# A gated graph network and an attention layer on one core: where the loads and the preparation of the weights stand in the order of work

## The chip, the cores and the metric

The kernel runs on one core of a Trainium2 chip. The metric is the device time of one execution in microseconds, here the median of three runs.

## The reference

The input holds 64 graphs of 256 nodes with 256 features each (x) and one integer adjacency matrix per graph (adj). Layer 0 is a gated graph network of three steps, layer 1 a graph attention network with four heads; each acts on a normalized copy of x and is added to x.

```python
h = relu(layernorm(x))
for i in range(3):                                  # layer 0
    m = h @ weight[i]
    aggr = A.T @ m                                  # per graph, A = (adj != 0)
    gi, gh = aggr @ w_ih.T + b_ih, h @ w_hh.T + b_hh
    r, z = sigmoid(i_r + h_r), sigmoid(i_z + h_z)   # thirds of gi and gh
    n = tanh(i_n + r * h_n)
    h = (1 - z) * n + z * h
x = x + h
h = relu(layernorm(x))                              # layer 1
v = h @ W.T + b                                     # 4 heads of 64
logits = leaky_relu(l_src[:, None] + l_dst[None, :], 0.2), masked where adj != 1
x = x + softmax(logits) @ v
```

Here l_src and l_dst are products of v with the two halves of a.

## The kernel before

Two graphs form a pair; there are 32 pairs. The work of a pair is cut into ticks: pair p begins at tick 18 p (APART), its step l of layer 0 has its six parts tick_0 to tick_5 at ticks 12 l to 12 l + 5 after that, and attention follows from tick 32. So two or three pairs are under way at a time, except at the beginning and the end. In ticks 6 to 11 only pair 0 is under way, and it has no step then: only its update (L499), its transposes back (L546) and the sums of its new state (L381).

The order of the work is written out by hand. `at(tick, phase, p, fn)` (L307) enters a function under a tick and one of the phases STEP, READY and REST; the last loop (L777) calls them by tick and phase, the later pair first, and in the order of entry within a pair. Nothing reorders the instructions afterwards: each engine runs its own in the order in which they were issued. TensorE (PE) does the products and transposes, VectorE (DVE) and ScalarE (ACT) evict PSUM and do the elementwise work, GpSimd (POOL) some of it, SyncE (SP) issues most loads. Three PSUM banks (`bank`, L97) go round among the transposes, the aggregation and the preparation of weights, five others among the gates.

DMAs issued on SP and ACT take eight completion counters in turn, in the order in which the program issues them. A DMA whose counter has been used waits, on the engine that issues it, until the earlier DMA of this counter has landed. ACT issues DMAs from the same stream of instructions that holds its evictions.

Before the ticks begin, the kernel issues the loads of x and adj of the first pair on SP (L123), and on ACT those of w_ih, weight[0], w_hh, the other weights and the two biases (L149 to L175). PE transposes w_ih and w_hh in blocks of 128 x 128 (L169), and DVE evicts them as ih_T and hh_T (L170). From hh_T DVE makes w_h (L196, L197) and seven blocks w_n (L198 to L205). `step_weights(l)` (L207) transposes weight[l] (pmT, L212; evicted by ACT, L215), multiplies it by ih_T (pc, L220; evicted by DVE, L224) and makes of it the six blocks of w_a[l] (RA, ZA, NA, S1, S2, S4; L226 to L229), which step l uses from its tick_2 on. `step_weights(0)` stands before the ticks, `step_weights(1)` at tick 6, `value_weights` (L238) at tick 7, `step_weights(2)` at tick 8. `value_weights` loads W, b and eight pieces of a, builds a_exp (the pieces as columns among zeros), w_val and b_val for the attention, which uses them from tick 37.

Of pair 0, `plan_norm` (L310) gives statistics of x (L320), rstd (L326, L327) and the normalized xn_a (L332); `plan_relu_T` transposes it (pt_a, L351) into hT_a (L352); `first_hi` (L535) and `first_lo` (L539) split it into hNhi and hNlo; `to_edge` (L526) makes the edge matrix; `state_sums` (L381) makes T1, T3n and T2n. tick_0 aggregates (pa, L418), tick_2 has the first product with w_a (p), tick_3 and later the products pd, pc, pe and pn. In the trace the tiles T1, T2, T3 and T4 are shown as T.

Of the kernel before, what the change touches and what calls it, by code (L numbers as in the profile page):

```python
# [17 lines left out]
P = 128  # L18
# [8 lines left out]
def gated_gnn_then_gat_kernel(  # L27
# [95 lines left out]
    first = load_x(0), load_adj(0, "adj")  # L123
# [23 lines left out]


    ih_T = [buf("val", [P, G * P], f"ih_T_{k}") for k in range(KD)]  # L149
    hh_T = [buf("row", [P, G * P], f"hh_T_{k}") for k in range(KD)]  # L150
    w_msgs = []
    for name, src, dst in (("ih", w_ih, ih_T), ("hh", w_hh, hh_T)):
        if name == "hh":
            w_msgs.append(buf("hn", [P, KD, D], "w_msg_0"))
            nc.scalar.dma_start(w_msgs[0], weight[0].rearrange("(k q) e -> q k e", q=P))
        nat = buf("zz", [P, G, D], f"{name}_nat")
        for g0 in range(0, G, 3):
            nc.scalar.dma_start(
                nat[:, g0 : g0 + 3, :], src[g0 * P : (g0 + 3) * P, :].rearrange("(g q) d -> q g d", q=P)
            )  # L160
        if name == "hh":
            for l in range(1, L):
                w_msgs.append(buf("row", [P, KD, D], f"w_msg_{l}"))
                nc.scalar.dma_start(w_msgs[l], weight[l].rearrange("(k q) e -> q k e", q=P))
        for k in range(KD):
            for g0 in range(0, G, 3):
# [3 lines left out]
                nc.vector.tensor_copy(dst[k][:, g0 * P : (g0 + 3) * P], pt[:, : 3 * P])  # L170

    bi = const.tile([P, G], F32, name="bi")
    bh = const.tile([P, G], F32, name="bh")
    nc.scalar.dma_start(bi, b_ih.rearrange("(g q) -> q g", q=P))
    nc.scalar.dma_start(bh, b_hh.rearrange("(g q) -> q g", q=P))  # L175
# [18 lines left out]
    for k in range(KD):  # L194
        r_, z_, n_ = (hh_T[k][:, ts(g, D)] for g in range(3))
        nc.vector.tensor_copy(w_h[:, k, ts(RH, D)], r_)  # L196
        nc.vector.tensor_sub(w_h[:, k, ts(RZ, D)], r_, z_)  # L197
        nc.vector.tensor_scalar_mul(w_n[:, (N00, N01)[k], :], n_[:, :P], 0.5)  # L198
        nc.vector.tensor_scalar_mul(w_n[:, (NS3, N11)[k], :], n_[:, P:], 0.5)
    nb = [w_n[:, j, :] for j in range(7)]  # L200
# [6 lines left out]
    def step_weights(l):  # L207
# [8 lines left out]
        for k in range(KD):  # L216
# [12 lines left out]
            nc.vector.tensor_scalar_mul(blk[ZA], blk[ZA], -1.0)  # L229

    step_weights(0)

    w_val = const.tile([P, KD, VW], F32, name="w_val")
    b_val = const.tile([P, VW], F32, name="b_val")

# [575 lines left out]
```

## Time and profile before

| | us |
|---|---|
| median of three runs (2610.36 to 2613.37) | 2613.26 |
| the profiled execution, whole | 2612.2 |
| its span | 2610.4 |
| PE busy in it | 2539.7 (97%) |
| DVE busy | 1849.2 (71%) |
| ACT busy | 1462.2 (56%) |
| POOL busy | 653.0 (25%) |
| first matmul of the first aggregation (pa, L418) | 39.22 |
| first product with w_a (p, L293) | 46.38 |

The profile is of one execution, and its times count from the start of the span. In a timeline a row gives start, duration, engine, line, operation, output and inputs with their shapes, the number of instructions taken together (x), and in brackets how long the engine had been idle before and what released it. PEld is PE's loading of weights, which overlaps its products. ACTq and SPq are rows of the queues, which issue DMAs. PEclk is the clock that PE was granted, as a share of full speed. In a table by stages each engine has its busy time and its instructions.

### The profile page before, as it was taken

Reading aid. Unit: us, or ns where it says so; the run is one execution under the profiler, and the core shown is the slowest. Engines: PE = TensorE matmul, PEld = TensorE weight load, DVE = VectorE, ACT = ScalarE, POOL = GpSimd, SP = SyncE. Lnnn points to the kernel's source line nnn. Section 1 sums busy time; section 2 is a strip of 40 time slices with the busy share of each in tenths; the row PEclk is TensorE's granted clock in tenths of the full one; section 3 lists DMA queues with packets and bytes.
Section 4 is the critical chain, followed back from the end, with each engine's and each line's share of the span. In section 5 each row is a group of like instructions: output and inputs, shape, how many; then the busy total and the mean of one; then the engine's idle time right before and its main releaser. Section 6 shows DMA issues by size and latency. Waiting matters only on the chain.

```text
span 2610.4 us, 38818 instructions
## 1 busy us (share of the span) xinstructions
PE 2539.7 (97%) x14074; PEld 2266.0 (87%) x14074; DVE 1849.2 (71%) x4528; ACT 1462.2 (56%) x3077; POOL 653.0 (25%) x518
## 2 busy tenths in 40 slices
PE   6899999999999999999999999999999999999985
PEld 5688898888988888989888989888898888898975
DVE  4567777777776777777777777777777677777663
ACT  2346555655655665655665555565565566565553
POOL 0012222222223222222222322222222322222221
PEclk9899999999999999999999999999999999999995
DMA  3004344434344434344443334443434453433444
GB/s 89 19 9 94 89 110 98 110 85 90 82 106 98 114 84 88 92 95 106 106 98 92 84 88 110 98 111 85 90 81 106 98 114 84 89 92 86 98 98 114
DMA packets 120320, 239.89 MB, mean 92 GB/s; under 512 B 9792, under 2 KB 79424, under 8 KB 120128
## 3 DMA queue, kind: packets, MB, share of 16 engines
q0 software_dynamic: 34272, 132.13, 26.5%
q1 hardware_dynamic: 80160, 102.52, 12.9%
q10 hardware_dynamic: 5696, 2.76, 0.4%
q8 instruction: 111, 1.82, 0.3%
q14 instruction: 81, 0.66, 0.1%
HBM read 219.82 MB, written 17.56 MB: 91 GB/s over the span
## 4 chain that ended last, share of the span: by engine, by line
PE 95%; DVE 2%; DMA 1%; issue 1%; ACT 0%; POOL 0%; ACTq 0%; POOLq 0%; SPq 0%; DVEq 0%
PE pd L293 19%; PE pn L293 13%; PE pc L293 13%; PE po L749 9%; PE pa L418 7%; PE qb L396 6%; PE pe L293 6%; PE p L293 6%; PE qa L396 5%; PE pv L601 4%; PE pback L552 3%; PE pt_a L351 1%; PE pt_b L351 1%; PE plink L652 1%; PE pc L220 0%
## 5 line engine op out<-in xcount | busy, mean ns | idle before, releaser
L487 POOL TENSOR_TENSOR R<-hT_a,hn 128x512 f32<-128x512 f32 x192 | 318.3, 1658 | 883.7 <-ACT hn L484 840.9
L293 PE MATMUL pn<-aggr,w_a 128*128 128x256 f32 x1536 | 367.1, 382 | 0.0
L293 PE MATMUL pd<-T,w_a 128*128 128x256 f32 x1536 | 364.6, 380 | 0.0
L293 PEld LDWEIGHTS pn<-aggr,w_a 128*128 128x128 f32 x1536 | 287.1, 190 | 42.9 <-DVE pn L473 6.3
L293 PEld LDWEIGHTS pd<-T,w_a 128*128 128x128 f32 x1536 | 286.9, 190 | 36.9
L749 PEld LDWEIGHTS po<-val,zz 128*128 128x128 f32 x2048 | 258.7, 201 | 17.2 <-ACT zz L740 12.5
L749 PE MATMUL po<-val,zz 128*128 128x65 f32 x2048 | 255.9, 281 | 11.6 <-ACT zz L740 11.6
L689 DVE CUSTOM_DVE_ANT_0 any<-drow,noedge 128x256 f32<-128x256 f32 x512 | 244.7, 478 | 16.9 <-DMA drow<-score_dram 7.9
L762 POOL TENSOR_TENSOR x<-x,o 128x256 f32<-128x256 f32 x128 | 117.1, 915 | 498.2 <-DVE o L757 498.2
L484 ACT ACTIVATE hn<-pn,bi 128x256 f32<-128x256 f32 x384 | 160.4, 469 | 144.5 <-PE pn L293 144.4
L403 ACT ACTIVATE R<-pc,brz 128x256 f32<-128x256 f32 x192 | 80.5, 470 | 280.0 <-PE pc L293 280.0
L717 ACT ACTIVATE zz<-zz,val 128x256 f32<-128x256 f32 x512 | 231.7, 509 | 8.3 <-DMA zz<-score_dram 8.3
L502 DVE SCALAR_TENSOR_TENSOR R<-Z,R 128x512 f32<-128x512 f32 x192 | 131.8, 686 | 147.3 <-POOL R L487 142.7
L558 DVE TENSOR_TENSOR hNlo<-pback,hNhi 128x512 fp32r<-128x512 f32 x128 | 88.5, 691 | 196.2 <-ACT hNhi L557 196.2
L403 ACT ACTIVATE R<-pe,brz 128x256 f32<-128x256 f32 x192 | 80.5, 470 | 195.2 <-PE pe L293 195.2
L503 DVE SCALAR_TENSOR_TENSOR hT_a<-R,hn 128x512 f32<-128x512 f32 x192 | 175.0, 912 | 13.6 <-DVE R L502 0.5
L293 PE MATMUL pc<-hT_a,w_h 128*128 128x256 f32 x768 | 181.4, 379 | 0.0
L293 PE MATMUL pe<-aggr,w_a 128*128 128x256 f32 x768 | 181.4, 379 | 0.0
L293 PE MATMUL pc<-aggr,w_a 128*128 128x256 f32 x768 | 181.4, 379 | 0.0
L293 PE MATMUL pd<-T,w_h 128*128 128x256 f32 x768 | 181.4, 379 | 0.0
L293 PE MATMUL p<-T,w_a 128*128 128x256 f32 x768 | 181.4, 379 | 0.0
L473 DVE SCALAR_TENSOR_TENSOR pn<-R,hn 128x512 f32<-128x512 f32 x192 | 142.9, 744 | 52.0 <-ACT hn L399 27.4
(147 smaller groups left out, 5310.6 us busy)
## 6 DMA issues: line engine op xcount, KB each, us to landing
zz<-score_dram POOLq DMA_DIRECT2D x64, 1024.0 KB, 11.9
zz<-topT_dram POOLq DMA_DIRECT2D x62, 1024.0 KB, 8.1
adj<-in_adj_dram SPq DMA_DIRECT2D x64, 512.0 KB
drow<-score_dram SPq DMA_DIRECT2D x64, 512.0 KB
x<-in_x_dram SPq DMA_DIRECT2D x32, 512.0 KB
out_dram<-x SPq DMA_DIRECT2D x32, 512.0 KB
score_dram<-score SPq DMA_DIRECT2D x128, 4.0 KB
topT_dram<-topT SPq DMA_DIRECT2D x128, 2.0 KB
```

The costliest lines, as they stand in the source:

```text
L293: nc.tensor.matmul(pt[:, ts(c, N)], w[:, k, j * D + c * P : j * D + (c + 1) * P], src[:, k, :], start=start and c == 0 and k == 0, stop=(c ...
L396: nc.tensor.matmul(pt, w_n[:, j, :], src, start=start, stop=True, skip_group_check=True)
L403: nc.scalar.activation(of(dst, i)[:, c, :], src[:, c, :], AF.Tanh, bias=brz[:, g0 + c : g0 + c + 1], scale=0.5)
L418: nc.tensor.matmul(pt[:, ts(i, N)], hN[half][:, i * KN + s, ts(e, P)], edge[:, i * KN + s, :], start=(s == 0 and half == 0), stop=(s == KN ...
L473: nc.vector.scalar_tensor_tensor(by_c(self.bank(f"pn{i}")), of(self.R, i), 1.0, of(self.hn, i), op0=ALU.add, op1=ALU.mult)
L484: nc.scalar.activation(n__[:, c, :], p_n[:, c, :], AF.Tanh, bias=bi[:, 2 * KD + c : 2 * KD + c + 1])
L487: nc.gpsimd.tensor_sub(of(self.R, i), of(self.hT(), i), n__)
L502: nc.vector.scalar_tensor_tensor(d_, of(self.Z, i), 1.0, d_, op0=ALU.add, op1=ALU.mult)
L503: nc.vector.scalar_tensor_tensor(of(self.hT(), i), d_, 0.5, of(self.hn, i), op0=ALU.mult, op1=ALU.add)
L689: nc.vector.tensor_tensor_reduce(any_, drow[r // KN][:, h, :], v["noedge"][:, r, :], 1.0, -3.0e38, ALU.add, ALU.max, accum_out=v["top"][:, ...
L717: nc.scalar.activation(zz[:, h, :], zz[:, h, :], AF.Prelu, alpha=ALPHA, bias=v["val"][:, r, S0 + H + h : S0 + H + h + 1],)
L749: nc.tensor.matmul(po[:, ts(h_, VC)], logits[i][:, j, h_, ts(s, P)], v["val"][:, i * KN + j, ts(h_, VC)], start=(j == 0), stop=(j == KN - 1),)
```

## The change

The loads move ahead of everything else. SP issues x_0, w_hh, adj_0, weight[0], w_ih, weight[1], weight[2] and W, and then the later loads of x and adj; ACT issues the two biases, then b, the eight pieces of a, and b once more. POOL clears a_exp and presets b_val. The preparation of the weights becomes functions at ticks: w_hh's (`state_weights`) at tick -5, on ACT in place of DVE, with its remaining DVE part (`state_weights_2`) at tick -2; w_ih's and the transposes of weight[0] at tick 0, `step_weights(0)` at tick 1; the transposes of weight[1] at tick 5 and `step_weights(1)` at tick 6; of weight[2] at tick 13 and `step_weights(2)` at tick 14; `value_weights` at tick 20, without its loads. In `turn_gates` and `step_weights` some of the evictions go to ACT. These functions are now entered after those of the pairs, so within a phase they follow those of pair 0.

```diff
--- before.py
+++ after.py
@@ -120,7 +120,35 @@
         return xt
     ctx.enter_context(tc.manual_schedule())
-    first = load_x(0), load_adj(0, "adj")
+    def load_gates(name, src):
+        nat = buf("zz", [P, G, D], f"{name}_nat")
+        for g0 in range(0, G, 3):
+            nc.sync.dma_start(
+                nat[:, g0 : g0 + 3, :], src[g0 * P : (g0 + 3) * P, :].rearrange("(g q) d -> q g d", q=P)
+            )
+        return nat
+    def load_square(tag, name, src):
+        y = buf(tag, [P, KD, D], name)
+        nc.sync.dma_start(y, src.rearrange("(k q) e -> q k e", q=P))
+        return y
+    x_0 = load_x(0)
+    hh_nat = load_gates("hh", w_hh)
+    first = x_0, load_adj(0, "adj")
+    ih_T = [buf("val", [P, G * P], f"ih_T_{k}") for k in range(KD)]
+    hh_T = [buf("row", [P, G * P], f"hh_T_{k}") for k in range(KD)]
+    w_msgs = [load_square("Z", "w_msg_0", weight[0])]
+    ih_nat = load_gates("ih", w_ih)
+    w_msgs += [load_square("row", f"w_msg_{l}", weight[l]) for l in range(1, L)]
+    w_nat = load_square("zz", "w_nat", W)
+    bi = const.tile([P, G], F32, name="bi")
+    bh = const.tile([P, G], F32, name="bh")
+    nc.scalar.dma_start(bh, b_hh.rearrange("(g q) -> q g", q=P))
+    nc.scalar.dma_start(bi, b_ih.rearrange("(g q) -> q g", q=P))
     ident = const.tile([P, P], F32, name="ident")
@@ -144,35 +172,14 @@
     mhalf = const.tile([P, R], F32, name="mhalf")
     nc.gpsimd.memset(mhalf, -0.5)
-    ih_T = [buf("val", [P, G * P], f"ih_T_{k}") for k in range(KD)]
-    hh_T = [buf("row", [P, G * P], f"hh_T_{k}") for k in range(KD)]
-    w_msgs = []
-    for name, src, dst in (("ih", w_ih, ih_T), ("hh", w_hh, hh_T)):
-        if name == "hh":
-            w_msgs.append(buf("hn", [P, KD, D], "w_msg_0"))
-            nc.scalar.dma_start(w_msgs[0], weight[0].rearrange("(k q) e -> q k e", q=P))
-        nat = buf("zz", [P, G, D], f"{name}_nat")
-        for g0 in range(0, G, 3):
-            nc.scalar.dma_start(
-                nat[:, g0 : g0 + 3, :], src[g0 * P : (g0 + 3) * P, :].rearrange("(g q) d -> q g d", q=P)
-            )
-        if name == "hh":
-            for l in range(1, L):
-                w_msgs.append(buf("row", [P, KD, D], f"w_msg_{l}"))
-                nc.scalar.dma_start(w_msgs[l], weight[l].rearrange("(k q) e -> q k e", q=P))
+    def turn_gates(name, nat, dst, evict):
         for k in range(KD):
             for g0 in range(0, G, 3):
                 pt = bank(f"pw_{name}_{k}_{g0}")
                 for g in range(3):
                     nc.tensor.transpose(pt[:, ts(g, P)], nat[:, g0 + g, ts(k, P)], ident)
-                nc.vector.tensor_copy(dst[k][:, g0 * P : (g0 + 3) * P], pt[:, : 3 * P])
-    bi = const.tile([P, G], F32, name="bi")
-    bh = const.tile([P, G], F32, name="bh")
-    nc.scalar.dma_start(bi, b_ih.rearrange("(g q) -> q g", q=P))
-    nc.scalar.dma_start(bh, b_hh.rearrange("(g q) -> q g", q=P))
+                evict[g0 // 3](dst[k][:, g0 * P : (g0 + 3) * P], pt[:, : 3 * P])
     brz = const.tile([P, 2 * KD], F32, name="brz")
@@ -191,63 +198,76 @@
     RH, RZ = range(2)
     N00, N01, N11, NS1, NS2, NS3, NS4 = range(7)
     RA, ZA, NA, S1, S2, S4 = range(6)
-    for k in range(KD):
-        r_, z_, n_ = (hh_T[k][:, ts(g, D)] for g in range(3))
-        nc.vector.tensor_copy(w_h[:, k, ts(RH, D)], r_)
-        nc.vector.tensor_sub(w_h[:, k, ts(RZ, D)], r_, z_)
-        nc.vector.tensor_scalar_mul(w_n[:, (N00, N01)[k], :], n_[:, :P], 0.5)
-        nc.vector.tensor_scalar_mul(w_n[:, (NS3, N11)[k], :], n_[:, P:], 0.5)
-    nb = [w_n[:, j, :] for j in range(7)]
-    nc.vector.tensor_add(nb[NS1], nb[NS3], nb[N11])
-    nc.vector.tensor_sub(nb[NS2], nb[NS1], nb[N00])
-    nc.vector.tensor_sub(nb[NS3], nb[N00], nb[NS3])
-    nc.vector.tensor_sub(nb[NS4], nb[N01], nb[NS2])
-    nc.vector.tensor_scalar_mul(nb[N11], nb[N11], -1.0)
-    def step_weights(l):
-        w_msgT = buf("zz", [P, KD, D], f"w_msgT_{l}")
+    def state_weights():
+        turn_gates("hh", hh_nat, hh_T, (nc.scalar.copy, nc.scalar.copy))
+        for k in range(KD):
+            r_, z_, n_ = (hh_T[k][:, ts(g, D)] for g in range(3))
+            nc.scalar.mul(w_n[:, (N00, N01)[k], :], n_[:, :P], 0.5)
+            nc.scalar.mul(w_n[:, (NS3, N11)[k], :], n_[:, P:], 0.5)
+            nc.scalar.copy(w_h[:, k, ts(RH, D)], r_)
+    def state_weights_2():
+        nb = [w_n[:, j, :] for j in range(7)]
+        nc.vector.tensor_add(nb[NS1], nb[NS3], nb[N11])
+        nc.vector.tensor_sub(nb[NS2], nb[NS1], nb[N00])
+        nc.vector.tensor_sub(nb[NS3], nb[N00], nb[NS3])
+        nc.vector.tensor_sub(nb[NS4], nb[N01], nb[NS2])
+        nc.vector.tensor_scalar_mul(nb[N11], nb[N11], -1.0)
+        for k in range(KD):
+            nc.vector.tensor_sub(w_h[:, k, ts(RZ, D)], hh_T[k][:, :D], hh_T[k][:, D : 2 * D])
+    w_msgT = {}
+    def step_weights_T(l):
+        w_msgT[l] = buf("zz", [P, KD, D], f"w_msgT_{l}")
         pt = bank(f"pmT_{l}")
         for e in range(KD):
             for k in range(KD):
                 nc.tensor.transpose(
                     pt[:, e * D + k * P : e * D + (k + 1) * P], w_msgs[l][:, k, ts(e, P)], ident
                 )
-        nc.scalar.copy(w_msgT.rearrange("q e d -> q (e d)"), pt)
+        nc.scalar.copy(w_msgT[l].rearrange("q e d -> q (e d)"), pt)
+    def step_weights(l):
         for k in range(KD):
             for g0 in range(0, G, 3):
                 pt = bank(f"pc_{l}_{k}_{g0}")
                 for e in range(KD):
                     nc.tensor.matmul(
-                        pt[:, : 3 * P], w_msgT[:, e, ts(k, P)], ih_T[e][:, g0 * P : (g0 + 3) * P],
+                        pt[:, : 3 * P], w_msgT[l][:, e, ts(k, P)], ih_T[e][:, g0 * P : (g0 + 3) * P],
                         start=(e == 0), stop=(e == KD - 1),
                     )
-                nc.vector.tensor_copy(w_a[l][:, k, g0 * P : (g0 + 3) * P], pt[:, : 3 * P])
+                (nc.scalar.copy if g0 else nc.vector.tensor_copy)(
+                    w_a[l][:, k, g0 * P : (g0 + 3) * P], pt[:, : 3 * P]
+                )
             blk = [w_a[l][:, k, ts(j, D)] for j in range(6)]
             nc.vector.tensor_add(blk[S1], hh_T[k][:, D : 2 * D], blk[ZA])
             nc.vector.tensor_sub(blk[S2], blk[S1], hh_T[k][:, :D])
             nc.vector.tensor_sub(blk[S4], blk[RA], blk[S2])
             nc.vector.tensor_scalar_mul(blk[ZA], blk[ZA], -1.0)
-    step_weights(0)
     w_val = const.tile([P, KD, VW], F32, name="w_val")
     b_val = const.tile([P, VW], F32, name="b_val")
     a_exp = const.tile([P, KD, 2 * H], F32, name="a_exp")
+    bcol = const.tile([P, KD], F32, name="bcol")
+    nc.scalar.dma_start(bcol, b.rearrange("(k q) -> q k", q=P))
+    nc.gpsimd.memset(a_exp, 0.0)
+    for h in range(H):
+        k, q0 = divmod(h * C, P)
+        for s in range(2):
+            nc.scalar.dma_start(
+                a_exp[q0 : q0 + C, k, s * H + h : s * H + h + 1],
+                a[h : h + 1, s * C : (s + 1) * C].rearrange("o c -> c o"),
+            )
+    nc.gpsimd.memset(b_val, 1.0)
+    nc.scalar.dma_start(
+        b_val[:, :S0].rearrange("q (h c) -> q h c", h=H)[:, :, :C],
+        bass.AP(tensor=b.tensor, offset=b.offset, ap=[[0, P], [C, H], [1, C]]),
+    )
     def value_weights():
-        w_nat = buf("zz", [P, KD, D], "w_nat")
-        nc.scalar.dma_start(w_nat, W.rearrange("(k q) d -> q k d", q=P))
-        bcol = const.tile([P, KD], F32, name="bcol")
-        nc.scalar.dma_start(bcol, b.rearrange("(k q) -> q k", q=P))
-        nc.vector.memset(a_exp, 0.0)
-        for h in range(H):
-            k, q0 = divmod(h * C, P)
-            for s in range(2):
-                nc.scalar.dma_start(
-                    a_exp[q0 : q0 + C, k, s * H + h : s * H + h + 1],
-                    a[h : h + 1, s * C : (s + 1) * C].rearrange("o c -> c o"),
-                )
         nc.vector.memset(w_val, 0.0)
         for k in range(KD):
             pt = bank(f"pwv_{k}")
@@ -264,11 +284,6 @@
                     start=(g == 0), stop=(g == KD - 1),
                 )
             nc.vector.tensor_copy(w_val[:, k, S0:], pa[:, : 2 * H])
-        nc.vector.memset(b_val, 1.0)
-        nc.scalar.dma_start(
-            b_val[:, :S0].rearrange("q (h c) -> q h c", h=H)[:, :, :C],
-            bass.AP(tensor=b.tensor, offset=b.offset, ap=[[0, P], [C, H], [1, C]]),
-        )
         bmat = buf("o", [P, KD, P], "bmat")
         pb = bank("pb")
         for k in range(KD):
@@ -768,12 +783,24 @@
             rest(t, output(r))
         rest(66, lambda: nc.sync.dma_start(out_rows[ts(p, T), :].rearrange("(r q) d -> q r d", q=P), v["x"]))
-    at(SUB, REST, 0, lambda: step_weights(1))
-    at(SUB + 1, REST, 0, value_weights)
-    at(SUB + 2, REST, 0, lambda: step_weights(2))
     for p in range(NPAIR):
         plan_pair(p)
+    at(-5, REST, 0, state_weights)
+    at(-2, READY, 0, state_weights_2)
+    def input_weights():
+        turn_gates("ih", ih_nat, ih_T, (nc.scalar.copy, nc.vector.tensor_copy))
+        step_weights_T(0)
+    at(0, REST, 0, input_weights)
+    at(1, REST, 0, lambda: step_weights(0))
+    at(5, REST, 0, lambda: step_weights_T(1))
+    at(SUB, REST, 0, lambda: step_weights(1))
+    at(13, REST, 0, lambda: step_weights_T(2))
+    at(14, REST, 0, lambda: step_weights(2))
+    at(20, REST, 0, value_weights)
     for tick in sorted(plan):
         for phase in plan[tick]:
             for _, fn in sorted(phase, key=lambda y: y[0]):
```

## The prediction

> **What bounds the kernel now.** I read the busy time by stages first. It asks where TensorE (PE) is idle, since only there can a new order of the work gain.
>
> ```profile
> core 0: us, PE busy (x) PEld busy (x) DVE busy (x) ACT busy (x) POOL busy (x), PEclk, DMA share, GB/s
> 0.00:36.30 36.30, 19.22 (x72) 13.14 (x72) 16.35 (x50) 2.70 (x5) 1.83 (x9) 0.94 0.46 137
> 36.30:60.40 24.10, 22.42 (x102) 19.57 (x102) 11.57 (x25) 9.65 (x21) 1.28 (x1) 0.88 0.08 23
> 60.40:92.80 32.40, 20.54 (x74) 13.81 (x72) 16.22 (x41) 3.35 (x7) 2.24 (x2) 0.79 0.06 13
> 92.80:120.00 27.20, 27.20 (x144) 24.36 (x145) 16.66 (x29) 13.68 (x30) 2.82 (x2) 1.00 0.13 39
> ```
>
> From 92.8 us PE is busy throughout at clock 1.00, and the page's chain of waits gives PE 95% of the span. So what is saved before 92.8 us reaches the end whole, and what is added to PE later is paid whole. Before 92.8 us PE idles 17.1 + 1.7 + 11.9 us and runs partly at a low clock. The timeline says why:
>
> ```profile
> 33.72 1.38 DVE L332 TENSOR_SCALAR xn_a<-x,mv_a,rstd_a 128x256 f32<-128x256 f32 x4 [1.24 <-POOL rstd_a L327]
> 38.38 0.69 DVE L526 TENSOR_SCALAR edge<-adj 128x1024 fp32r<-128x1024 int32 x1
> 39.22 0.55 PE L418 MATMUL pa<-edge,hNhi_a 128*128 128x256 f32 x1 [1.68 <-DVE edge L526]
> 46.38 1.89 PE L293 MATMUL p<-T,w_a 128*128 128x256 f32 x8
> ...
> 69.84 5.04 ACTq L247 DMA_DIRECT2D a_exp<-in_L_gnn_a_dram  x8
> 74.16 0.57 PE L262 MATMUL pwa<-a_exp,w_nat 128*128 128x8 f32 x2 [6.33 <-DMA a_exp<-in_L_gnn_a_dram]
> ...
> 82.55 7.37 PE L220 MATMUL pc<-ih_T,w_msgT 128*128 128x384 f32 x16 [0.68 <-ACT w_msgT L215]
> 92.75 0.39 PE L418 MATMUL pa<-edge,hNlo 128*128 128x256 f32 x1 [1.33 <-DVE hNlo L558]
> ```
>
> The first aggregation (pa) starts at 39.22 us because DVE normalizes x_0 only after all weights (x_0's statistics start at 30.06). PE goes from the end of step 0 (60.41) to the aggregation of step 1 (92.75) through all remaining weights, with a wait for the 4-byte loads of a_exp. DMAs that wait for a completion counter show in ScalarE's queue:
>
> ```profile
> 5.03 3.21 ACTq L158 DMA_DIRECT2D hh_nat<-in_L_gnn_w_hh_dram  x2
> 10.68 3.39 ACTq L164 DMA_DIRECT2D w_msg<-in_L_gnn_weight_dram  x2
> 16.66 0.38 ACTq L174 DMA_DIRECT2D bi<-in_L_gnn_b_ih_dram  x1
> 17.07 0.56 ACTq L175 DMA_DIRECT2D bh<-in_L_gnn_b_hh_dram  x1
> ```
>
> By the program's waits, the first hh_nat may issue when x_0 has landed, which therefore was at 5.03. The gaps in this queue are such waits.
>
> **What the Trainium skill says.** "DMA: Bandwidth & Descriptors", section "Issuing engines are not separate DMA queues": transfers of all issuers share the same 16 DMA engines. The trace agrees: from 4 to 5 us SP's queue alone moved 0.35 MB, from 6 to 7 us the two queues 0.17 and 0.18. Its section "Queues, rings and completion order" has an engine alternate between queues packet by packet; these equal shares agree. "Perfetto Trace Analysis", section "DMA Instruction — HWDGE (DVE, Sync)": the semaphore wait lies on the issuing sequencer, ahead of the start that is reported, and the sequencer is free only after the issue. The gaps above agree; that work of ScalarE's own (ACT) queues behind such a wait, no row shows yet. "TensorE: Matmul & The Clock Gate", section "What's actually happening": half clock by default and after about 3.4 us of idleness. The products of L220 agree: loads every 0.64 us after 20.11 and again after 82.55, every 0.31 from 86.53.
>
> **Part 1, loads.** SP now issues x_0, w_hh, adj_0, weight[0], w_ih, weight[1], weight[2], W, x_1 in that order, and ACT issues b_hh, b_ih, b, eight pieces of a, and b again: 12 small DMAs ahead of its first evictions. Eight counters are used in turn, so ACT's sequencer meets these waits: b behind b_ih; the eight pieces of a behind w_hh, adj_0, both halves of w_ih, b, piece 1, weight[2], W; the last DMA behind piece 3. Then the hh_T evictions may go. I time W, the latest of them. SP's first bytes up to 3.0 us are 0.066 MB, then 0.348 MB/us. Up to W there are 3.67 MB: 3.0 + 3.60/0.348 = 13.4 us. The two bias loads are 1,536 packets, 96 per DMA engine. Packets of this kind took 21 ns of an engine alone (775 in the us from 18 to 19) at a share of 0.41, so between 0.8 and 2.0 us; I take 1.3. Receipt 1.1 us (x_1's last byte was at about 9.4 by the counts, seen at 10.68; x_0 took 0.7). W is seen at 15.8. Then one piece of a (5.04/8 = 0.63) and 0.38 for the last: ACT is free at c = 16.8 us, 15 to 20 with the ends (a late b_hh also holds the second half of w_ih on SP).
>
> **Part 2, up to the first aggregation.** From c, on ACT: four copies of 384 columns (0.48 each, between 0.39 for 256 and 0.59 for 512; the fourth waits for PE's transposes into a bank that the first frees, 0.87) 1.9 us, four products and two copies 1.4, hT_a, hNhi and the hand over 1.6. On DVE: hNlo 1.14, the five small operations of w_n 1.08 (22.01 to 23.09), two subtractions 0.66, edge to pa 0.84. Sum 8.6: pa at 25.4. x_0's normalization now waits for b_ih (brz comes first on DVE; seen by 10.4) and then takes 5.0 us (30.06 to 35.1), done by 16: hidden behind ACT.
>
> **Part 3, within step 0.** From pa to p (the first product with w_a) are 7.16 us now. PE gets in between 12 + 4 transposes (0.54 per four) 2.2, 16 records of L220 at 0.32, 5.1, and a wait of about 0.2 for DVE's S1 of the second half, behind ACT's copy: 7.5. So p at 25.4 + 7.16 + 7.5 = 40.1 where it was at 46.38: **6.3 us gained**. If the clock falls to half in between, up to 3 less.
>
> **Part 4, between step 0 and step 1.** Up to the last product of weights 1 nothing changes on PE (60.41 to about 67.2, at the old times). DVE decides: after the update (64.44) copy 0.56, about 0.4 until ACT's copy is there, four operations 1.47; then copy 0.56, until ACT's copy at 68.0, 1.47, two hNlo 1.3: 70.75. So 10.35 us in place of 32.34: **22.0 gained**, between 20.5 and 22.5. Late next is DVE, with PE idle about 1.6 us there.
>
> **Part 5, given back.** weights 2 moves into ticks 13 and 14, where PE is full: 0.54 + 5.1 = **5.6**; its DVE and ACT parts have slack there (DVE is 61% busy from 92.8 to 120). value_weights moves to tick 20. PE's own part is about 1.8 us, but there are three banks: pwv_1 waits for the eviction of hNlo (1.6 us after the transposes), pwa_1 for the memset and copy on DVE, pb for bmat behind all of them (copies 0.42, 0.17, 0.42, 0.17, then 0.29). On PE 4.15 us pass until the next product: **4.2**, between 1.8 and 6. Queued behind PE's wait is pd of pair 1, and behind it all of PE's later work. Where DVE catches up sooner, less is paid. SP is moved past eight more issues, of x_1 at about 13 us; it lands by 19, and is first read in tick 4 (54.5 now, some 48 then): nothing. POOL's two memsets replace DVE's: nothing.
>
> **The sum.** 6.3 + 22.0 − 5.6 − 4.2 = 18.5 us. The profiled execution took 2612.2 us (span 2610.4), so it would be 2593.7; against the median of 2613.26, 1.1 above it, **2594.8 us**.
>
> **Rivals.** *A, as above: 2594.8.* *B, ACT's own work isn't held by its DMA waits*, or they end early. Then DVE decides: b_ih at 10.4, then the old 9.16 us from the statistics to pa, 1.74 more for the new operations: pa at 21.4, 4 us sooner: 2590.8; with the biases at 7 us, 2588. For it: no row shows ACT's work held. Against: the sequencer's waits in ACTq are real. *C, the moved weights cost more than their place saves*: the products at half clock (0.64, 5.1 more) and value_weights at 6 instead of 4.2: 2601.7. For it: the cold L220 rows; against: PE is at 1.00 wherever these now stand, and idle gaps of 1 us (61.2 to 62.2) left it warm. *D, slower: ACT's small DMAs run one after another*, each a full round trip. That is decided from the point at which ACT is free at 35.3 us (16.8 + 18.5). A piece of a took 2.3 us from issue to use, the second bias load 2.9; with 0.5 for contention, 12 × 3.4 + 0.75 = 41.6 us, so 6.3 us slower: 2619.6. Against: the counters chain at most three of them. *E, it does nothing:* excluded for part 4, since the wait for a_exp at 74.16 has no work left behind it; only a price in part 5 of the size of the gain could bring it about.
>
> **How the numbers follow.** A 0.61, B 0.17, C 0.13, E or a weak D within 0.2% 0.05, D 0.04. About 0.2% (5 us) is what a measurement of this kernel can tell from no change. The range 2588 to 2603 takes in A with its bounds (c 3 us later, value_weights at 1.8 or 6), B and C. Faster 0.91, same 0.05, slower 0.04.
>
> **What would show it.** ACT's first copy of hh_T between 15 and 19 us, directly after b_val's issue (B: at about 9); pa near 25, p near 40; the first wait of PE for hNlo in step 1 near 64; products of weights 2 at 0.32 us a record in a full PE; a gap of 2 us around pwv and pb at tick 20; thereafter each row about 18.5 us earlier. The prediction is wrong if the rows after 120 us move by another amount than the rows before.

## The result, and the profile after

| | before | after |
|---|---|---|
| median, us | 2612.61 (4 runs, 2610.36 to 2613.37) | 2596.09 (4 runs, 2595.86 to 2596.36) |
| profiled execution, whole / span | 2612.2 / 2610.4 | 2595.86 / 2594.1 |
| PE busy in it | 2539.7 | 2532.7 |

The ratio is 0.9938, with a 95% interval from 0.9921 to 0.9955: 16.5 us faster by the medians, 16.3 by the two spans. 2594.8 was forecast.

From L169 on most line numbers of the changed kernel are higher than before, by 11 to 20 (L293 is now L308, L418 is L433, L558 is L573). First the busy time by stages, cut where the first aggregation, the first product with w_a, the aggregation of step 1 and the end of what follows tick 20 now lie; each engine has its busy time and its instructions, then come the clock, the share of the DMA engines and GB/s.

```profile
core 0: us, PE busy (x) PEld busy (x) DVE busy (x) ACT busy (x) POOL busy (x), PEclk, DMA share, GB/s
0.00:25.60 25.60, 8.56 (x42) 6.42 (x43) 8.03 (x27) 6.81 (x16) 2.13 (x11) 1.00 0.72 210
25.60:41.00 15.40, 15.38 (x67) 12.34 (x68) 6.68 (x15) 5.01 (x10) 0.00 (x0) 1.00 0.11 35
41.00:65.00 24.00, 21.77 (x99) 17.14 (x97) 14.95 (x36) 9.05 (x21) 3.52 (x3) 1.00 0.00 1
65.00:106.00 41.00, 39.05 (x201) 33.23 (x202) 25.80 (x53) 16.87 (x36) 2.82 (x2) 1.00 0.09 26
106.00:120.00 14.00, 14.00 (x61) 12.09 (x61) 7.62 (x18) 5.44 (x14) 1.28 (x2) 0.88 0.01 1
```

Before the first aggregation PE idled 18.7 us (39.2 less 20.5 busy), now 17.0; and that stretch ends at 25.6 instead of 39.2. Between step 0 and the aggregation of step 1 the long idle is gone (2.2 us from 41 to 65). New is an idle of 2 us in 65 to 106, and a clock of 0.88 after it, in a stretch where PE is busy throughout. (The 1.00 of the first two rows leaves out what the clock's record does not cover at the beginning: up to 30.7 us the matmuls go at half rate.)

The timeline of the same kernel, at the places that were shown of before:

```profile
7.93 0.37 ACTq L255 DMA_DIRECT2D bcol<-in_L_gnn_b_dram  x1
8.01 0.16 DVE L186 TENSOR_TENSOR brz<-bi,bh 128x4 f32<-128x4 f32 x1 [6.23 <-DMA bi<-in_L_gnn_b_ih_dram]
8.41 8.00 ACTq L260 DMA_DIRECT2D a_exp<-in_L_gnn_a_dram  x8
16.50 0.54 ACTq L265 DMA_DIRECT2D b_val<-in_L_gnn_b_dram  x1
17.09 1.24 ACT L181 COPY hh_T<-pw_hh 128x384 f32<-128x384 f32 x3 [13.68 <-issue]
...
25.62 0.55 PE L433 MATMUL pa<-edge,hNhi_a 128*128 128x256 f32 x1 [3.41 <-DVE edge L541]
40.95 1.89 PE L308 MATMUL p<-T,w_a 128*128 128x256 f32 x8
64.95 0.39 PE L433 MATMUL pa<-edge,hNlo 128*128 128x256 f32 x1 [1.26 <-DVE hNlo L573]
73.44 5.33 PE L236 MATMUL pc<-ih_T,w_msgT 128*128 128x384 f32 x16
100.39 0.38 PE L275 MATMUL pwv<-ident,w_nat 128*128 128x128 f32 x2
102.02 0.44 PE L275 MATMUL pwv<-ident,w_nat 128*128 128x128 f32 x2 [0.90 <-DVE hNlo L573]
103.11 0.61 PE L282 MATMUL pwa<-a_exp,w_nat 128*128 128x8 f32 x4 [0.66 <-DVE w_val L276]
104.12 0.61 PE L292 MATMUL pb<-a_exp,bmat 128*128 128x8 f32 x4 [0.39 <-DVE bmat L290]
104.58 2.58 PE L308 MATMUL pd<-T,w_a 128*128 128x256 f32 x8
106.95 3.02 PE L308 MATMUL pc<-aggr,w_a 128*128 128x256 f32 x8
```

ACT's first copy of hh_T comes 0.05 us after the last of its small DMAs was issued, and the profile finds nothing else that it waited for ("issue", after 13.68 us of no work). Read one by one, the pieces of a were issued at 8.41, 9.83, 11.69, 12.90, 13.99, 14.51, 15.15 and 15.80. Of the 9.1 us from 7.93 to 17.05, the ten issues themselves are 5.2 and the waits between them 3.9; from 13.99 on the issues follow each other without a wait. pa starts at 25.62, p at 40.95, and PE waits for hNlo in step 1 until 64.95. weights 2 go at 0.33 us a record in a full PE. Around value_weights PE pauses three times (0.90, 0.66, 0.39). The pd behind it and the next pc take 2.58 and 3.02 us where eight products of this form take 1.89 otherwise (the row of p).

Where the time went is read from one instruction that every step has, DVE's addition pe (L457 before, L472 after). The table gives its start before, and by how many us each kernel has it earlier. In the order of the columns it lies behind the beginning, behind the way to step 1 and weights 2, and behind tick 20.

| | pair 0, step 0 | pair 0, step 1 | pair 1, step 0 | fifth | next to last | last | span |
|---|---|---|---|---|---|---|---|
| start before | 50.10 | 102.21 | 123.93 | 167.14 | 2485.13 | 2519.61 | 2610.4 |
| changed kernel | 5.42 | 21.43 | 16.73 | 15.65 | 15.62 | 16.25 | 16.3 |
| e1, small loads on SP | 12.03 | 28.04 | 23.94 | 23.94 | 23.94 | 24.02 | 23.5 |
| e2, value_weights in pieces | 5.43 | 21.43 | 21.28 | 19.84 | 19.83 | 20.43 | 20.9 |
| e3, weights 2 at tick 8 | 5.47 | 21.40 | 16.20 | 15.44 | 15.43 | 15.16 | 15.5 |
| e4, before with a loaded early | 0.61 | 6.63 | 6.62 | 6.62 | 6.62 | 6.49 | 7.5 |
| e5, e1 and e2 together | 11.94 | 27.96 | 27.81 | 26.36 | 26.37 | 26.38 | 27.8 |
| e6, the beginning alone | 11.98 | 12.29 | 12.29 | 12.29 | 12.29 | 12.56 | 13.5 |
| e7, value_weights at tick 21 | 5.63 | 21.64 | 21.82 | 18.69 | 18.70 | 18.65 | 18.7 |
| e8, value_weights at tick 7 | 6.52 | 17.54 | 17.72 | 17.71 | 17.72 | 18.07 | 18.7 |

For the changed kernel: the beginning gains 5.42; the way to step 1, with weights 2 paid, 16.01; tick 20 and what follows takes back 5.78; then the distance stays at 15.6 for 2300 us, and the end adds 0.6. What is won or lost before about 130 us stays unchanged up to the next to last pe; behind it the distances change once more, by up to 1.4 us (e5 shows most of the reason).

### The profile page after: what moved, and what is told of

Read it like the earlier page. It is cut to its first block, busy times and chain, and to the rows that moved or that the text cites. A ratio compares the mean times of both kernels' runs of the same rounds, so it can differ in the third digit from the quotient of the medians.

```text
span 2594.1 us, 38817 instructions
## 1 busy us (share of the span) xinstructions
PE 2532.7 (98%) x14074; PEld 2264.3 (87%) x14074; DVE 1841.0 (71%) x4508; ACT 1470.2 (57%) x3095; POOL 653.5 (25%) x520
## 3 DMA queue, kind: packets, MB, share of 16 engines
q1 hardware_dynamic: 82848, 105.14, 13.1%
## 4 chain that ended last, share of the span: by engine, by line
PE 95%; DVE 2%; DMA 1%; issue 1%; ACT 1%; POOL 0%; ACTq 0%; POOLq 0%; SPq 0%; DVEq 0%
PE pd L308 19%; PE pn L308 13%; PE pc L308 13%; PE po L764 9%; PE pa L433 7%; PE qb L411 6%; PE pe L308 6%; PE p L308 6%; PE qa L411 5%; PE pv L616 4%; PE pback L567 3%; PE pt_b L366 1%; PE pt_a L366 1%; PE pc L236 1%; PE plink L667 1%
## 5 line engine op out<-in xcount | busy, mean ns | idle before, releaser
L308 PE MATMUL pn<-aggr,w_a 128*128 128x256 f32 x1536 | 367.1, 382 | 0.0
L308 PE MATMUL pd<-T,w_a 128*128 128x256 f32 x1536 | 365.3, 381 | 0.0
L308 PEld LDWEIGHTS pn<-aggr,w_a 128*128 128x128 f32 x1536 | 287.6, 190 | 42.5 <-DVE pn L488 6.3
L308 PEld LDWEIGHTS pd<-T,w_a 128*128 128x128 f32 x1536 | 287.6, 191 | 36.8
L418 ACT ACTIVATE R<-pc,brz 128x256 f32<-128x256 f32 x192 | 80.6, 470 | 283.7 <-PE pc L308 283.7
L573 DVE TENSOR_TENSOR hNlo<-pback,hNhi 128x512 fp32r<-128x512 f32 x128 | 88.4, 692 | 194.9 <-ACT hNhi L572 194.9
L418 ACT ACTIVATE R<-pe,brz 128x256 f32<-128x256 f32 x192 | 80.6, 470 | 195.1 <-PE pe L308 195.1
L308 PE MATMUL pc<-aggr,w_a 128*128 128x256 f32 x768 | 182.6, 381 | 0.0
L308 PE MATMUL pc<-hT_a,w_h 128*128 128x256 f32 x768 | 181.5, 379 | 0.0
L308 PE MATMUL pd<-T,w_h 128*128 128x256 f32 x768 | 181.5, 379 | 0.0
L308 PE MATMUL pe<-aggr,w_a 128*128 128x256 f32 x768 | 181.4, 379 | 0.0
L308 PE MATMUL p<-T,w_a 128*128 128x256 f32 x768 | 181.4, 379 | 0.0
```

Of the source, the lines that this page charges most:

```text
L308: nc.tensor.matmul(pt[:, ts(c, N)], w[:, k, j * D + c * P : j * D + (c + 1) * P], src[:, k, :], start=start and c == 0 and k == 0, stop=(c ...
L418: nc.scalar.activation(of(dst, i)[:, c, :], src[:, c, :], AF.Tanh, bias=brz[:, g0 + c : g0 + c + 1], scale=0.5)
```

## The experiments

The theory to test is A of the prediction: ACT is held by its own small DMAs; the loads of a_exp and DVE set the gap between the steps; the moved work is paid where it goes. Each experiment is measured against the kernel before, run on the same chip.

**e1: the small loads on SP.** The changed kernel, with the loads of b and a issued by the other engine:

```diff
-    nc.scalar.dma_start(bcol, ...)
+    nc.sync.dma_start(bcol, ...)
...
-            nc.scalar.dma_start(
+            nc.sync.dma_start(
                 a_exp[q0 : q0 + C, k, s * H + h : s * H + h + 1],
...
-    nc.scalar.dma_start(
+    nc.sync.dma_start(
         b_val[:, :S0].rearrange("q (h c) -> q h c", h=H)[:, :, :C],
```

> The changed kernel with the eight pieces of a and the two loads of b issued on SP behind W, in place of ACT; nothing else. Theory A (ACT's evictions stand behind the waits of its own small DMAs, and so set the first aggregation): ACT's first copy of hh_T moves from 17.1 us to about 8, the first aggregation is then set by DVE's normalization and comes at about 19.2 us in place of 25.6, and the time falls by 6.4 us to about 2589.7. Rival B (ACT is not held by those waits; w_hh, PE or DVE set the start): pa stays near 25.6 and the time near 2596.1.

Measured: 2589.19 us (2588.72 to 2589.35), ratio 0.9913 (0.9899 to 0.9926). Its timeline:

```profile
7.59 0.48 ACT L181 COPY hh_T<-pw_hh 128x384 f32<-128x384 f32 x1 [4.18 <-PE pw_hh L180]
9.83 6.28 SPq L260 DMA_DIRECT2D a_exp<-in_L_gnn_a_dram  x8
18.72 0.55 PE L433 MATMUL pa<-edge,hNhi_a 128*128 128x256 f32 x1 [3.42 <-DVE edge L541]
```

The same eight loads now hold SP, and ACT waits for nothing but PE's transposes: its first copy is at 7.59 instead of 17.09, pa at 18.72 instead of 25.62. The beginning gains 12.03 us instead of 5.42. So in the changed kernel 6.6 us of the beginning are lost to ACT's DMA issues and the waits between them. The Trainium skill's page "Perfetto Trace Analysis", section "DMA Instruction — HWDGE (DVE, Sync)", puts a DMA's semaphore wait on the sequencer that issues it; this pair of traces agrees, and adds that ACT's own work stands behind it.

**e2: value_weights in pieces.** The same operations in six functions, each in a tick of its own (the comments say what each holds):

```diff
-    at(20, REST, 0, value_weights)
+    at(20, REST, 0, value_ready)           # w_val cleared, bmat
+    at(21, REST, 0, lambda: value_T(0))    # pwv_0 and its eviction
+    at(22, REST, 0, lambda: value_T(1))
+    at(23, REST, 0, lambda: value_a(0))    # pwa_0 and its eviction
+    at(26, REST, 0, lambda: value_a(1))
+    at(28, REST, 0, value_b)               # pb and its eviction
```

> The changed kernel with the weights of the attention prepared in pieces: the memset and bmat at tick 20, the two transposes at ticks 21 and 22, the products with a at 23 and 26, the one for b at 28. Same instructions. Theory A (most of the cost at tick 20 is PE's waiting for banks and for bmat, 2.0 us, and the half clock of 3.4 us that follows the thin stretch, 1.7 us): 3.5 us less, about 2592.6, and no stretch at half clock after 60 us. Rival C (the cost is PE's own work, or the half clock comes from elsewhere): within 1 us of 2596.1.

Measured: 2591.09 us (2590.92 to 2591.68), ratio 0.992 (0.9907 to 0.9934). The distance falls from 21.43 to 19.83 only: 1.6 us for what costs 5.78 at tick 20. PE has no pause there and stays at clock 1.00 up to the end region, so the stretch at half clock is gone, as theory A said. The time is 1.5 us better than its 2592.6.

**e3: weights 2 back at tick 8.**

```diff
-    at(13, REST, 0, lambda: step_weights_T(2))
-    at(14, REST, 0, lambda: step_weights(2))
+    at(SUB + 2, REST, 0, lambda: step_weights_T(2))
+    at(SUB + 2, REST, 0, lambda: step_weights(2))
```

> The changed kernel with the transposes and products of weight[2] at tick 8, the tick of the kernel before, in place of ticks 13 and 14. Theory A (between step 0 and step 1 DVE sets the pace, so the weights of step 2 cost about 5 us there, as they cost 5.6 in ticks 13 and 14, and the gain of that stretch comes from elsewhere): within 1.5 us of 2596.1. Rival F (moving these weights to a tick where other work runs is itself what pays): slower by 4 to 6 us, about 2601.

Measured: 2596.54 us (2595.99 to 2596.66), ratio 0.994 (0.9928 to 0.9952). The pe of step 1 is earlier by 21.40, as in the changed kernel (21.43). Moving weights 2 gains nothing by itself: PE pays for them in a full tick or between the steps.

**e4: the kernel before, with W, b and a loaded early.** The loads and presets of `value_weights` move from tick 7 to the place after `step_weights(0)`; everything else is the kernel before.

```diff
     step_weights(0)
...
+    w_nat = buf("zz", [P, KD, D], "w_nat")
+    nc.scalar.dma_start(w_nat, W.rearrange("(k q) d -> q k d", q=P))
+    bcol = const.tile([P, KD], F32, name="bcol")
+    nc.scalar.dma_start(bcol, b.rearrange("(k q) -> q k", q=P))
+    nc.vector.memset(a_exp, 0.0)
+    for h in range(H):
...
     def value_weights():
-        w_nat = buf("zz", [P, KD, D], "w_nat")
```

> The kernel before, with the loads of W, b and the pieces of a, and the two memsets that go with them, ahead of the ticks (behind step_weights(0)) and the rest of value_weights left at tick 7; all weights where they were. Theory A (the wait for the pieces of a, with the half clock that follows it, is most of the gain between step 0 and step 1): 7 us of wait and 2.6 us of half clock go, about 9.5 us less than the kernel before, 2603. Rival F (the ticks at which the weights are prepared make that gain): within 2 us of the kernel before, 2612.6.

Measured: 2604.95 us (2601.54 to 2606.91), ratio 0.9971 (0.996 to 0.9982). Its timeline:

```profile
67.12 0.61 PE L268 MATMUL pwa<-a_exp,w_nat 128*128 128x8 f32 x4
...
75.24 8.05 PE L220 MATMUL pc<-ih_T,w_msgT 128*128 128x384 f32 x16 [0.68 <-ACT w_msgT L215]
```

pwa is done at 67 us, without a wait, where before it came at 74.16. The gain in the trace is 6.0 us between the steps (6.63 − 0.61), less than expected: weights 2 still run mostly at half clock (8.05 us for 16 records, 7.37 before), and PE now pauses 2.23 us for DVE ahead of the second pwa. So the late loads of a_exp were 6 of the 32 us between the steps. Rival F is refuted; but 6.0 us is not most of what the stretch lost in the changed kernel, so theory A as it was put is not borne out by this run (e6 and e8 come back to it). The six times of this kernel scatter by 5.4 us.

**e5: e1 and e2 in one kernel.**

> Both edits in one kernel: the ten small loads of b and a issued on SP, and value_weights in six pieces at ticks 20 to 28. Alone they gave 2589.19 and 2591.09 where the changed kernel takes 2596.09. If each takes away a wait of its own, they add up except for the stretch at half clock, which each of them lost: 2589.19 less the 2.5 us that the pieces save on PE (4.1 to 1.6) is 2586.7. Rival: the two share one cause, so that the second gives nothing more: 2589. First aggregation at 18.7 us in both cases; PEclk 1.00 from 25 us to the end region.

Measured: 2584.14 us (2583.69 to 2584.42), ratio 0.9891 (0.9877 to 0.9904): the best of all, 12 us below the changed kernel. The distance in the trace is 26.37, which is e1's beginning (12.0) plus 16.0 between the steps less 1.6 for value_weights. So the two causes are separate. It is 2.6 us faster than expected, and the spans put 1.9 of it behind the last pe, where both kernels have the same instructions in the same order: from there to the end e1 takes 91.3 us, e5 89.4. First e1, then e5, from the last pe to the end:

```profile
2495.60:2586.90 91.30, 56.55 (x271) 50.09 (x269) 41.82 (x128) 32.35 (x60) 18.94 (x19) 0.63 0.48 110
```

```profile
2493.20:2582.60 89.40, 53.67 (x263) 47.84 (x262) 41.89 (x129) 32.35 (x60) 19.23 (x19) 0.65 0.48 111
```

The addition pe runs on DVE, and PE is not equally far when it starts: 271 products are left or under way in e1, 263 in e5. So the stretch is better measured on PE. Its 400th product or transpose from the end starts 120.2 us before the end in e1, 118.4 in e5; the 350th 107.2 and 106.9. Between the two e1 has an interval at half clock, where e5 stays at 1.00. First e1, then e5:

```profile
2475.20:2478.60 3.40, 3.27 (x7) 2.50 (x8) 1.21 (x3) 1.66 (x3) 1.21 (x1) 0.50 1.04 201
```

```profile
2475.00:2500.00 25.00, 23.06 (x140) 20.64 (x138) 13.87 (x40) 13.25 (x22) 3.89 (x4) 1.00 0.94 196
```

Of the ten kernels of the table, four have such an interval there (the kernel before, e1, e3 and e7) and need 13.0 to 13.1 us for these fifty; the other six have none and need 11.4. So 1.6 of the 1.9 us are this interval.

**e6: the beginning alone.** Loads, state_weights and weights 0 as changed; `value_weights` with its own loads of b and a again at tick 7, weights 1 and 2 at ticks 6 and 8.

```diff
-    at(5, REST, 0, lambda: step_weights_T(1))
+    at(SUB, REST, 0, lambda: step_weights_T(1))
...
-    at(20, REST, 0, value_weights)
+    at(SUB + 1, REST, 0, value_weights)
```

> The beginning of the changed kernel alone: the loads, state_weights and weights 0 as changed, but b and the pieces of a loaded inside value_weights at tick 7, and weights 1 and 2 at ticks 6 and 8, as before the change. Theory A (the small loads held ACT in the changed kernel, and the time from step 0 to step 1 is another matter): first aggregation at 18.7, 12.0 us gained there, nothing gained between the steps where PE waits for a_exp again: 2600. Rival (the start is worth 5.4 us, whatever ACT issues): 2606.5.

Measured: 2598.5 us (2596.94 to 2598.89), ratio 0.9945 (0.9931 to 0.9958). Its timeline:

```profile
58.38 5.24 ACTq L262 DMA_DIRECT2D a_exp<-in_L_gnn_a_dram  x8
62.69 0.57 PE L277 MATMUL pwa<-a_exp,w_nat 128*128 128x8 f32 x2 [6.41 <-DMA a_exp<-in_L_gnn_a_dram]
65.38 0.60 PE L277 MATMUL pwa<-a_exp,w_nat 128*128 128x8 f32 x2 [2.12 <-DMA a_exp<-in_L_gnn_a_dram]
```

The beginning gains 11.98 us, as in e1, since ACT has no small loads ahead of its copies; the way to step 1 gains nothing (12.29 there), since PE waits for a_exp again (6.41 + 2.12). So in the changed kernel the early loads of a_exp spare PE this wait between the steps, and cost 6.6 us at the beginning, on ACT.

**e7: value_weights at tick 21**, one line changed (20 to 21).

> The changed kernel with value_weights at tick 21 instead of 20. PE is full there too. If the stretch at half clock after value_weights (3.4 us, some 1.6 us lost) comes from where its pauses happen to fall, it may vanish or stay: 2594.5 or 2596.1, and the pauses of PE around pwv and pb remain some 2.5 us in either case. Rival (the pauses depend on what stands ahead on DVE at that tick): they shrink below 1 us, 2592.

Measured: 2593.46 us (2593.43 to 2594.03), ratio 0.9927 (0.9915 to 0.994). Its timeline:

```profile
103.64 0.38 PE L275 MATMUL pwv<-ident,w_nat 128*128 128x128 f32 x2
104.22 0.42 PE L275 MATMUL pwv<-ident,w_nat 128*128 128x128 f32 x2
105.22 0.61 PE L282 MATMUL pwa<-a_exp,w_nat 128*128 128x8 f32 x4 [0.58 <-DVE w_val L276]
106.22 0.61 PE L292 MATMUL pb<-a_exp,bmat 128*128 128x8 f32 x4 [0.39 <-DVE bmat L290]
106.69 0.68 PE L411 MATMUL qb<-T4n,w_n 128*128 128x256 f32 x2
```

The pause of 0.90 for hNlo is gone, since no eviction of hNlo stands ahead at this tick; the two others stay. 3.05 us pass on PE instead of 4.19, and PE stays at full clock. That 2.5 us of pauses would remain was wrong; 0.97 remain. The rival is right that they depend on what stands ahead on DVE, though its 2592 is 1.5 us too low.

**e8: value_weights at tick 7, with the early loads kept**, one line changed (20 to SUB + 1).

> The changed kernel, its early loads kept, with value_weights back at tick 7. Theory A (only the loads of a_exp made it dear at tick 7; the gap between the steps has about 1.6 us of idle PE and is bound by DVE): it costs there its work on DVE and PE, 3 to 5.5 us, and saves 4.3 us and the stretch at half clock at tick 20, so 2593.2 to 2595.7, first aggregation of step 1 at 68 to 70.5 instead of 64.95. Rival (the gap can hide it in its idle PE): 2590. Rival (pauses there bring half clock over the following steps): over 2598.

Measured: 2593.49 us (2593.25 to 2595.89), ratio 0.9928 (0.9916 to 0.9941). Its timeline:

```profile
63.85 0.44 PE L275 MATMUL pwv<-ident,w_nat 128*128 128x128 f32 x2 [1.54 <-DVE hNlo L573]
64.94 0.61 PE L282 MATMUL pwa<-a_exp,w_nat 128*128 128x8 f32 x4 [0.65 <-DVE w_val L276]
65.94 0.96 PE L292 MATMUL pb<-a_exp,bmat 128*128 128x8 f32 x4 [0.39 <-DVE bmat L290]
68.15 0.78 PE L433 MATMUL pa<-edge,hNhi 128*128 128x256 f32 x1
```

The way to step 1 with weights 2 gains 11.02 (17.54 − 6.52) instead of 16.01: value_weights cost 5.0 us there, against 5.78 at tick 20. So the idle PE between the steps doesn't hide them. PE waits for DVE three times (1.54, 0.65, 0.39), and then an interval at half clock follows, in which it is busy throughout, which at half rate is up to 1.7 us lost:

```profile
66.00:69.40 3.40, 3.40 (x15) 3.22 (x16) 1.08 (x4) 0.94 (x2) 0.00 (x0) 0.51 0.02 5
```

The second rival was right about this interval, though not about its size. The move to tick 20 is worth nothing: with the loads early, the old place is as good or better. 1.1 us of this kernel's lead over the changed one lie in the beginning (6.52 against 5.42), where both have the same code; there PE's clock rises at 28.5 us instead of 30.7, and that part is no effect of the edit. With e6 this kernel also says what the early loads are worth once the rest is changed. Between the two lie these loads and the ticks of weights 1 and 2 (those of weights 2 are worth nothing by e3), and the way to step 1 gains 0.31 there and 11.02 here. So of the 16.0 us some 10.7 come with the early loads, where e4, which adds them to the old order, gains 6.0; the other 5.0 come from moving value_weights out of the gap, and are paid again at tick 20.

**e9 to e12: the same pauses, shifted against the clock.** In all these traces the changes of PE's clock lie whole multiples of 3.413 us apart. In the changed kernel the interval from 105.8 to 109.2 us is at half clock:

```profile
99.00:102.40 3.40, 2.50 (x18) 2.05 (x16) 2.77 (x6) 1.44 (x3) 0.00 (x0) 1.00 0.00 0
102.40:105.80 3.40, 2.35 (x15) 2.08 (x15) 1.56 (x8) 0.00 (x0) 0.00 (x0) 1.00 0.00 0
105.80:109.20 3.40, 3.40 (x10) 2.69 (x9) 1.96 (x4) 0.00 (x0) 0.00 (x0) 0.50 0.00 0
109.20:112.60 3.40, 3.40 (x17) 3.01 (x16) 1.13 (x2) 1.20 (x3) 0.00 (x0) 1.00 0.00 0
```

e1 has the same three pauses (0.90, 0.66, 0.39), and no such interval:

```profile
92.70:96.10 3.40, 2.25 (x16) 1.79 (x14) 2.67 (x7) 1.44 (x3) 0.00 (x0) 1.00 0.00 0
96.10:99.50 3.40, 2.60 (x15) 2.36 (x16) 1.36 (x7) 0.00 (x0) 0.00 (x0) 1.00 0.00 0
99.50:102.90 3.40, 3.40 (x18) 2.99 (x17) 1.96 (x4) 1.19 (x3) 0.00 (x0) 1.00 0.00 0
```

Is that a matter of where the pauses fall in the intervals? The first product of pair 1's step 0 was repeated, which sets the rest of PE's work later:

```diff
-            self.part(q_a[:, :N], N00, h0[:, 0, :], start=True)
+            for _ in range(2 if self.n_ == "1_0" else 1):   # 2, 4, 6 or 9
+                self.part(q_a[:, :N], N00, h0[:, 0, :], start=True)
```

> The changed kernel with the first product of pair 1's step 0 done twice at tick 18, a repetition that only sets the rest 0.43 us later on PE. The pauses around value_weights at tick 20 stay as they are (PE 4.28 us from pwv to pd). Phase theory (PE's clock is decided at fixed instants 3.413 us apart, and the stretch at half clock comes only if the pauses fall suitably): the stretch comes or not: 2596.5 or 2594.8. Rival (these pauses always bring it): 2596.5, and 0.43 us later in the trace than in the changed kernel.

> As the run before, four times the same product, 1.29 us later. Phase theory: 2597.4 with the stretch at half clock, 2595.7 without it, and at least one of the three smaller shifts is without it. Rival: 2597.4, the stretch 1.29 us later.

> Six times the same product, 2.15 us later. Phase theory: 2598.2 with the stretch at half clock, 2596.6 without. Rival: 2598.2.

> Nine times the same product, 3.44 us later, nearly one whole interval between the instants at which the clock changes. Phase theory: the stretch at half clock is there again as in the changed kernel, one interval later: 2599.5. If another cause than phase took it away in the smaller shifts, it is absent here too: 2597.9. Rival (always there): 2599.5 as well, so this run counts only beside the other three.

Measured: 2596.22 (ratio 0.9939, 0.9926 to 0.9951), 2597.72 (0.9944, 0.9931 to 0.9958), 2599.01 (0.9948, 0.9936 to 0.9961) and 2598.87 us (0.995, 0.9937 to 0.9962). The pauses are the same in all four, and each has an interval at half clock behind them; the second has two in a row:

```profile
100.60:104.00 3.40, 1.84 (x16) 1.52 (x14) 2.59 (x7) 1.11 (x3) 0.00 (x0) 1.00 0.00 0
104.00:107.40 3.40, 3.01 (x11) 2.56 (x11) 0.60 (x4) 0.00 (x0) 0.00 (x0) 0.50 0.00 0
107.40:110.80 3.40, 3.40 (x10) 2.68 (x9) 1.48 (x3) 0.00 (x0) 0.00 (x0) 0.50 0.00 0
```

That at least one shift would be without it was wrong, and the rival's times came out. But the shifts didn't vary what they were meant to vary: the intervals lie differently in each execution, and the beginnings differ by up to 1 us as well (the clock first rises between 28.9 and 31.6 us). The first pwv comes 1.40 us after the start of its interval in the changed kernel, 2.50, 0.29, 2.86 and 2.13 in the four, 1.09 in e1. And the pauses don't always bring it, since e1 has the same ones. It isn't PE's busy time of the interval ahead that decides: 2.25 of 3.40 us brought no half clock in e1, 2.35 did in the changed kernel.

What does separate them can be counted in the timelines: the columns of the fp32 products and transposes with 128 or more columns that PE starts in an interval, those of the aggregation counted half, since they follow each other every 0.12 us and the others of 256 columns every 0.22. From the interval of the first pwv on, the changed kernel has 2048 and then 1536 such columns, e1 has 1792 and 1792: the same sum, divided at another place. In e9 to e12 the interval ahead of the first half clock has 512, 768, 256 and 768. In the first 130 us of all fourteen traces, from where the clock is recorded, 26 intervals with 1536 columns or fewer are all followed by half clock, and 382 with 1792 or more by full clock; of three with 1664, one by half clock. An interval full of these products at full clock has some 4096. So where the pauses fall does matter, through this count. It was made after the runs, and none of them set it on purpose. Behind 2440 us it has exceptions (4 of 560 intervals).

Nor does one trace stand for all executions of a kernel: of e11's five times four lie between 2598.84 and 2599.54, and one is 2596.68, where 2596.6 was expected without the stretch. Only one of the four was traced, so what the fifth did is not known.

## Why the prediction was right

The forecast was 2594.8 us, the median is 2596.09, within the range. The mechanism was A, and the sum came out 2.2 us too high (18.5 against 16.3 by the spans).

- **Part 1, loads.** ACT free at 16.8: its first copy is at 17.09. e1 shows that this is a hold by the DMAs, not late transposes. But the number was met by another path, and so in part by luck. Part 1 had the last wait end with W, seen at 15.8; the counters of the trace have W at 15.21, when ACT was still busy issuing. The last wait that held it was the one for b, a small load of its own, at 13.99 (6.0 us after its issue began); four issues without a wait followed. Part 1 had priced one piece and b_val there. The biases were seen at 8.01, not at 10.4: this changes nothing, since xn_a is hidden behind ACT either way.
- **Part 2.** pa at 25.4: 25.62.
- **Part 3.** p at 40.1: 40.95, so 5.4 us gained and not 6.3. From pa to p 15.33 us pass instead of 14.66. PE's clock rises only at 30.7 us, 5.1 us behind the start of pa, where before it rose at 42.1, 2.9 us behind it. Thirteen of the sixteen matmuls of pa ran at half rate (0.21 us apart) before too; what is new is that the products behind pa and the first transposes of w_ih do. 2.2 us more at half rate are 1.1 us lost, by this estimate; that possibility was named ("up to 3 less") and came true with 0.7.
- **Part 4.** 22.0 gained, 5.6 given back for weights 2, so 16.4: 16.01 measured. The wait for hNlo until 64.95 stands where it was forecast ("near 64"), and DVE is what is late. e4, e6 and e8 show of what it is made: the early loads of a_exp bring 6.0 us in the old order (e4) and some 10.7 in the new one (e6 against e8), and the other 5 us are value_weights itself (e8), its waits for DVE and its interval at half clock. What the sharing of the evictions with ACT is worth by itself was not tried. e4 corrects one belief: the half clock in weights 2 did not come from the wait for a_exp alone; without that wait it was still there.
- **Part 5.** weights 2 5.33 for 16 records (0.33 each, PE full, at full clock): as forecast. value_weights: 4.15 forecast, 4.19 measured from pwv to pd, with the three waits named. **The term that was mis-sized is what these waits do to the clock.** Part 5 took PE at 1.00 wherever the moved work stands; the ground for it stands under rival C, that a gap of 1 us had left the clock at 1.00 elsewhere (61.2 to 62.2 before). With three pauses in 4.2 us it was not: 3.4 us at half clock followed, so pd and pc take 0.7 and 1.1 us longer, and the cost of tick 20 is 5.78, near the upper bound of 6 that was kept for the range. That is 1.6 of the 2.2 us missing. The other terms: −0.9 in part 3, −0.35 in part 4, +0.6 at the end, which was taken as unchanged (there the kernel before has an interval at half clock that the changed one has not, see e5).
- **The rivals.** B (ACT not held) would have had its first copy at about 9 and 2590.8: refuted by the row at 17.09, and e1, which takes the hold away, shows what B's world costs: 2589.19. C was right in part, in that value_weights did lower the clock; weights 2 stayed at full clock. D (small DMAs one after another) did not occur: the eight pieces of a were issued in 8.0 us, 1.0 each, not at a round trip each. E did not occur.

Of "what would show it", the end fails: later rows are 15.6 us earlier, not 18.5. At 80 us the distance is 21.43; less the 4.2 of tick 20 it would be 17.2, and the rest is the clock. The last sign, that rows before and after 120 us move alike, fails with it: 16.73 at 107 us, 15.65 at 151, since part of what the clock costs falls between.

## What to carry to other kernels

An engine that issues DMAs and also does work on the critical path pays for every issue of its DMAs and for every wait between them: give small loads to a queue whose engine has nothing to do (6.6 us here), and look in the queue's rows for a long group directly ahead of its first instruction. A short chain between PE and another engine costs PE its round trips, not its work: split over ticks so that every link is done when its turn comes, the same operations cost 1.6 us instead of 5.8. And price pauses in a busy PE with the clock in mind: 2 us of pauses can bring a whole interval of 3.4 us at half clock, worth 1.7 us more, or two of them. Whether they do hangs here on how they fall into the intervals, so two kernels with the same pauses can differ by it.

## What the runs showed of the hardware that was not expected

The Trainium skill, "TensorE: Matmul & The Clock Gate", section "What's actually happening", gives a free-running activity window, about 3.4 us, and half clock after a window of idleness. The window agrees: the changes of the clock lie multiples of 3.413 us apart. The idleness doesn't, as a condition: no interval around value_weights was idle, and one with PE busy 2.35 of 3.40 us was followed by half clock. The measurement decides: pauses far shorter than the window are enough. What separates the intervals here is the count of columns under e9 to e12, with the change between 1536 and 1792 of some 4096, both on the way down and on the way up: an interval at half clock with 2048 columns (105.8 to 109.2 in the changed kernel) was followed by full clock. Why the clock follows it, the runs don't show, nor whether it holds for products of other kinds. Near the end of the kernel, where PE waits a good deal, an interval at half clock comes in some kernels and not in others, with the same products there, which then take 13.1 us instead of 11.4: a comparison of 2 us on this kernel has to look there first.
